# A graph network of four layers on one core: separate buffers for the attention outputs that the second attention projection loads, and v stored tile by tile

## The chip, the cores and the metric

The kernel runs on one core of one Trainium2 chip. The metric is the device time of one execution in microseconds (us), and lower is better. Times are medians of several executions. One further execution is recorded by the hardware profiler; the profile and the trace show that one.

## What is computed

The input is x with 2708 rows and 512 columns, and a symmetric 0/1 adjacency matrix of 2708 x 2708. Four layers follow each other, each as x = layernorm(x + layer(x)). Layers 0 and 1 sum neighbours through dense matrix products. Layers 2 and 3 are graph attention:

```python
def _layernorm(x):
    return (x - mean(x)) / sqrt(var(x) + 1e-5)

def gat_heads(x, adj, W, a):                    # W: [heads, 512, width]
    Wh  = einsum('nf,hfo->hno', x, W)           # the projection
    src = einsum('hno,ho->hn', Wh, a[:, :width])
    dst = einsum('hno,ho->hn', Wh, a[:, width:])
    e   = leaky_relu(src[:, :, None] + dst[:, None, :], 0.2)
    return softmax(where(adj > 0, e, -9e15)) @ Wh    # the attention, per head

# layer 2: 8 heads of 64
x = _layernorm(x + concat_heads(gat_heads(x, adj, W2, a2)))
# layer 3: 8 heads of 64, then one head of 512, then a two-layer MLP
h = elu(concat_heads(gat_heads(x, adj, W1, a1)))
h = elu(gat_heads(h, adj, Wo[None], ao[None])[0])
x = _layernorm(x + relu(h @ lin1_w + lin1_b) @ lin2_w + lin2_b)
```

## The kernel before

**Tiles and stages.** The 2708 rows are cut into NT = 22 tiles of 128 rows (the last has 20). The attention outputs are made in two blocks of 11 tiles each; `cuts` are their bounds. In time the kernel runs the layers 0 and 1 (to 889 us), the projection of layer 2 (889 to 981) and its attention (to 1531), the first projection of layer 3 (1531 to 1644) and its attention (to 2190), the projection to the single head of 512 (2190 to 2283; called layer 4's projection here), and its attention with the MLP (to 3004).

**The projection.** `project` is one function for all three projections. It loops over the 22 row tiles. For each tile t it takes the 128 rows of its input in SBUF from a function `source`, turns them with four TensorE transposes into PSUM (L124), copies these with ScalarE into a buffer `xT` (L126), and multiplies with the weight `w`: 16 matmuls (L627; four parts of the depth, twice over two halves of the columns) into the PSUM pair `pm`, of which there are two pairs. Of the two, 512 columns are Wh; 8 more columns in each half are the products with the attention vectors. From `pm` VectorE copies the `dst` column (L632) and a limited `src` column `b` (L634). ScalarE makes exponentials of them, `ecol` and `ucol` (L648, L649), VectorE multiplies Wh by `ecol` into the resident array `R2` (two L656; for the single head ScalarE does this), and ScalarE and GpSimd make `vcol` (L662) and `bcol` (L663). At the last tile of a block `split` cuts the block's exponentials into parts of lower precision (L560 to L564, L669, L672; some are casts on VectorE).

**The row v.** The attention needs exp of `b` as a row along the free axis, for all 128 partitions. `keep_v(t)`, called one tile late, transposes `b` (L604), takes the exponential with ScalarE into a row buffer `vrow` (L605), and at the last tile of a block stores this block's row to `v_dram` (L608, on SyncE's queue). The attention loads `v_bc` from there, a row of a block repeated on 128 partitions (`Weights.load`, L697, on SyncE's queue, 704 KB each). `Weights.first` is called by the projection at each tile: at tile NT - 8 it asks for two of these loads, and at tiles NT - 6 to NT - 3 it makes the first four arrays `e` of the attention (L703, VectorE), ordered by explicit dependencies between two tiles' products. Each `e` then gets its counterpart `c` by a sigmoid on ScalarE (L730), and the attention's matmuls are L895. At the end of each group of heads the attention stores its outputs to `o_dram` (L846, L848), and it stores the reciprocal sums in `rcs`.

**The source of layer 3's projection.** For layer 2 `source` is `plain`: it loads a tile of x2. For layer 3 it is `summed`: a load of the attention's outputs `o` (`fetched`, L164, 256 KB on SyncE's queue) and of x2 into a ring `spare` of two, then on VectorE o x rcs (L934) and + x2 (L935), and the layer norm in place:

```python
nc.vector.tensor_mul(by_head, by_head, rcs[...])              # L934
nc.vector.tensor_add(o, o, x2)                                # L935
layer_norm(late, o, n, o, on_scalar=True)
nc.gpsimd.dma_start(x3_dram[t * P:t * P + n, :], o)           # L937
return o
```

`layer_norm` computes statistics on VectorE (L108, L110, L112), takes the power -1/2 on GpSimd (L113), one more small step on VectorE (L117), and applies scale and bias with ScalarE (L118). The result x3 goes to `x3_dram` (L937, on GpSimd's queue) for the last layer's sum, and to the transposes L124. For layer 4's projection `elu_turned` loads the outputs already transposed, in pairs of tiles from tile 3 on, so that no transposes on TensorE are needed; SyncE issues these loads too.

**Buffers.** The pool `ahead` lives through the whole kernel. `fetched` takes its tiles there under the name `rows`, a ring of three, so that in layer 3's projection each `rows` buffer holds a tile from its load of o until its store of x3 and its transposes have ended. `xT` has two buffers in the same pool. The pool `sm` of a projection has two buffers of each name, unless told otherwise; `vrow` has one.

**Order.** The kernel is written as one program with all tiles' steps in a row. `early(first, n, make)` calls for the source of a tile one tile, and for its transposes none, ahead of the loop, and `xTs(t + 1)` is asked for ahead of tile t's matmuls. From that a scheduler makes one fixed list of instructions for each engine, and it sees the buffers: a step may be listed ahead only as far as there is a buffer for it. Each engine then executes its list in order, waiting on semaphores where data or a buffer are not ready; a DMA is started by the engine in whose list it stands. VectorE's list in layer 3's projection alternates between the steps of a tile's source (L934, L935 and the norm) and those that empty `pm` (L634, L632, L656). In the kernel before the source is three tiles ahead.

Of the kernel before, what the change touches and what calls it, by code (L numbers as in the profile page):

```python
# [9 lines left out]
F32 = mybir.dt.float32  # L10
# [3 lines left out]
AF = mybir.ActivationFunctionType  # L14
# [4 lines left out]
P = 128  # L19
D = 512  # L20
KD = D // P
EPS = 1e-5
ALPHA = 0.2
# [7 lines left out]
def kernel(  # L31
# [9 lines left out]
    nc = tc.nc  # L41
# [8 lines left out]
    def rows(t):  # L50
        return min(P, N - t * P)
# [34 lines left out]
    x2_dram = dram.tile([N, D], F32, name="x2_dram")  # L86
    x3_dram = dram.tile([N, D], F32, name="x3_dram")


    o_dram = dram.tile([N, D], F32, name="o_dram")  # L90
# [15 lines left out]
    def layer_norm(pool, y, n, dst, on_scalar=False):  # L106
        st = pool.tile([P, 6], F32, name="ln_st")
        nc.vector.bn_stats(st[:n], y)  # L108
        mv = pool.tile([P, 2], F32, name="ln_mv")
        nc.vector.bn_aggr(mv[:n], st[:n])  # L110
        rs = pool.tile([P, 1], F32, name="ln_rs")
        nc.vector.tensor_scalar(rs[:n], mv[:n, 1:2], EPS, None, op0=OP.add)  # L112
        nc.gpsimd.tensor_tensor(rs[:n], rs[:n], half[:n], OP.pow)  # L113
        if not on_scalar:
            nc.vector.tensor_scalar(dst, y, mv[:n, 0:1], rs[:n], op0=OP.subtract, op1=OP.mult)
            return
        nc.vector.scalar_tensor_tensor(mv[:n, 0:1], mv[:n, 0:1], -1.0, rs[:n], op0=OP.mult, op1=OP.mult)  # L117
        nc.scalar.activation(dst, y, AF.Identity, bias=mv[:n, 0:1], scale=rs[:n])  # L118
# [22 lines left out]
    ahead = fast.enter_context(tc.tile_pool(name="ahead", bufs=2))  # L141
# [7 lines left out]
    def early(first, n, make):  # L149

        made = {}

        def get(i, **how):
            for j in range(len(made), min(i + first + 1, n)):
                made[j] = make(j, **how)
            return made[i]
        return get
# [4 lines left out]
    def fetched(src, t, n, pool=ahead, name="rows", bufs=None):  # L162
        x_ = pool.tile([P, D], F32, name=name, bufs=bufs or (3 if pool is ahead else None))
        nc.sync.dma_start(x_[:n], src[t * P:t * P + n, :])  # L164
        return x_[:n]
# [28 lines left out]
    with ExitStack() as phase:  # L194
# [17 lines left out]
        sm = phase.enter_context(tc.tile_pool(name="l01", bufs=2))  # L212
# [22 lines left out]
        cuts = [(b, min(b + 4, NT)) for b in range(0, NT, 4)]  # L235
        cuts = cuts[-1:] + cuts[:-1]
# [38 lines left out]
        with ExitStack() as ph:  # L275
# [21 lines left out]
            for t in range(NT):  # L297
                n = rows(t)
# [29 lines left out]
        with ExitStack() as ph:  # L328
# [121 lines left out]
            for i, b in enumerate(cuts):  # L450
# [19 lines left out]
                for t in ts_:  # L470
                    n = rows(t)
# [9 lines left out]
            for t in range(NT):  # L481
                n = rows(t)
# [10 lines left out]
        with ExitStack() as ph:  # L493
            st = ph.enter_context(tc.tile_pool(name="l1b", bufs=2))
            for t in range(NT):
                n = rows(t)
# [17 lines left out]
    late = fast.enter_context(tc.tile_pool(name="late", bufs=1))  # L514
# [51 lines left out]
    def project(name, source, layer, v_dram, cuts, turned=None, first=None):  # L566


        w_src, w_view, _, heads = atts[layer]
# [9 lines left out]
        with ExitStack() as ph:  # L579
            sm = ph.enter_context(tc.tile_pool(name=f"{name}_s", bufs=2))  # L580
# [3 lines left out]
                           for k in (("pv", "pmm") if first else ("pmm", "pv")))  # L584
            if not first:
                ps_v, ps_mm = ps_mm, ps_v
            width = max(z - a for a, z in cuts) * P
            xs = early(1, NT, lambda t: source(sm, t, rows(t)))
            xTs = early(0, NT, lambda t: transposed(ahead, ps_tr, xs(t), rows(t), "xT"))
            if turned:  # L590
# [1 line left out]
                cuts_ = [(t, t + 1) for t in range(3)] + [(t, min(t + 2, NT)) for t in range(3, NT, 2)]  # L592
                parts = early(2, len(cuts_), lambda i: ready[i] if i in ready else turned(sm, *cuts_[i]))
                xTs = lambda t: parts(t if t < 3 else (t - 3) // 2 + 3)[:, :, ((t - 3) % 2 if t > 2 else 0) * P:][:, :, :P]
            vrows, bs, scaled = {}, {}, {}

            def keep_v(t):
                n = rows(t)
                a, z = next(c for c in cuts if c[0] <= t < c[1])
                if t == a:  # L600
                    vrows[a] = sm.tile([heads, width], F32, name="vrow", bufs=1)
                vrow = vrows[a]
                ps = ps_v.tile([P, P], F32, name="ps_v")
                nc.tensor.transpose(ps[:heads, :n], bs[t][:n, :heads], ident[:n, :n])  # L604
                nc.scalar.activation(vrow[:, (t - a) * P:(t - a) * P + n], ps[:heads, :n], AF.Exp, scale=ALPHA - 1.0)  # L605
                if t == z - 1:
                    cols = slice(a * P, a * P + (z - 1 - a) * P + n)
                    nc.sync.dma_start(v_dram[:, cols], vrow[:, :cols.stop - cols.start])  # L608

            for t in range(NT):  # L610
                n = rows(t)
# [17 lines left out]
                if t:  # L629
                    keep_v(t - 1)  # L630
# [34 lines left out]
                a, z = next(c for c in cuts if c[0] <= t < c[1])  # L665
                if t == z - 1:
                    if heads > 1:
# [3 lines left out]
                        for k in range(2):  # L671
                            nc.vector.tensor_scalar(pairs_c[:, a:z, :, k, 6 * k:6 * k + 3], parts_m[:, a:z, k::2, :],  # L672
                                                    -1.0, None, op0=OP.mult)
                            split(sm, pairs_c[:, a:z, :, k, 6 * k + 3:6 * k + 6], ecol[:, a:z, k::2])
            keep_v(NT - 1)
            sq = sm.tile([P, NT * H], F32, name="sq", bufs=1)[:, :NT * heads]
            dd = dcol[:, :, :heads]
# [56 lines left out]
    cuts = [-((-NT * i) // nb) for i in range(nb + 1)]  # L734
# [193 lines left out]

    def summed(sm, t, n):

        o, x2 = fetched(o_dram, t, n), fetched(x2_dram, t, n, late, "spare", 2)
        b = next(i for i, (a, z) in enumerate(blocks) if a <= t < z)
        by_head = o.rearrange("p (h c) -> p h c", h=H)
        nc.vector.tensor_mul(by_head, by_head, rcs[:n, b, :, t - blocks[b][0], None].to_broadcast([n, H, HO]))  # L934
        nc.vector.tensor_add(o, o, x2)  # L935
        layer_norm(late, o, n, o, on_scalar=True)
        nc.gpsimd.dma_start(x3_dram[t * P:t * P + n, :], o)  # L937
        return o

    loads, ready = [], {}  # L940

# [148 lines left out]
    for i, source in enumerate((plain, summed)):  # L1090
        with ExitStack() as ph:
            att = Weights(ph, f"a{2 + i}", blocks, vd[i])
            project(f"p{2 + i}", source, i, vd[i], blocks, first=att.first)
            heads_attention(f"a{2 + i}", att, i == 0, {
                9 + 4 * t: [lambda t=t: ready.update({t: elu_turned(None, t, t + 1)})] for t in range(3)} if i else {})
    ph4 = fast.enter_context(ExitStack())
    att = Weights(ph4, "a4", quads, vd[2])
    lin = ph4.enter_context(tc.tile_pool(name="lin", bufs=1)).tile([P, KD * FF + KF * D + KD * 512], F32, name="lin")
    scaled = project("p4", None, 2, vd[2], quads, elu_turned)


# [13 lines left out]
    def general(ctx):  # L1115
# [184 lines left out]
        def heads_attention(name, add):  # L1300

            with ExitStack() as ph:
# [51 lines left out]
                for b in range(nb):  # L1354
                    bc = att.load_shifts(b, 0)
                    for h in range(H):
                        nxt = att.load_shifts(b, h + 1) if h + 1 < H else None
                        main(b, h, bc, att.ahead(b + 1, h))
                        bc = nxt

        project("p2", lambda sm, t, n: None, l2_w, head_weights, head_vectors(l2_a), H)
        heads_attention("a2", add=True)
        project("p3", norm_and_keep, l3_w1, head_weights, head_vectors(l3_a1), H)
# [63 lines left out]
```

## Time and profile before

| | us |
|---|---|
| median of 3 runs | 3004.74 |
| lowest and highest | 3001.74, 3009.93 |
| profiled execution: its own time | 3005.91 |
| its span in the trace | 3004.1 |
| busy in the span: TensorE matmul (PE) | 2890.8 (96%) |
| TensorE weight load (PEld, beside PE) | 1608.9 (54%) |
| VectorE (DVE) | 1997.4 (66%) |
| ScalarE (ACT) | 1533.7 (51%) |
| GpSimd (POOL) | 251.0 (8%) |
| mean granted TensorE clock, 1 is full speed | 0.994 |

Busy times are sums over the whole span, while the stages differ: over the two attentions with 8 heads VectorE is nearly as busy as TensorE, in the projections it is not. The shares of a stage are therefore read from windows of the trace. A line of such a window has the start and end, the length, and for each engine its busy time and, in brackets, its number of instructions. In lines of the chain of waits and of the timeline, the first number is the start in us from the beginning of the span, the second the length; `out<-in` names what is written and read, and L12 is line 12 of the kernel. The trace leaves out the digits of names, so `x_dram<-rows` is here a store to `x3_dram`. SPq is SyncE's issuing of a DMA.

### The profile page before, as it was taken

Reading aid. Unit: us, or ns where it says so; the run is one execution under the profiler, and the core shown is the slowest. Engines: PE = TensorE matmul, PEld = TensorE weight load, DVE = VectorE, ACT = ScalarE, POOL = GpSimd, SP = SyncE. Lnnn points to the kernel's source line nnn. Section 1 sums busy time; section 2 is a strip of 40 time slices with the busy share of each in tenths; the row PEclk is TensorE's granted clock in tenths of the full one; section 3 lists DMA queues with packets and bytes.
Section 4 is the critical chain, followed back from the end, with each engine's and each line's share of the span. In section 5 each row is a group of like instructions: output and inputs, shape, how many; then the busy total and the mean of one; then the engine's idle time right before and its main releaser. Section 6 shows DMA issues by size and latency. Waiting matters only on the chain.

```text
span 3004.1 us, 36497 instructions
## 1 busy us (share of the span) xinstructions
PE 2890.8 (96%) x14456; PEld 1608.9 (54%) x14456; DVE 1997.4 (66%) x2405; ACT 1533.7 (51%) x1774; POOL 251.0 (8%) x341
## 2 busy tenths in 40 slices
PE   7999999999999999999998999999989999999998
PEld 3447766448888333444466334434465555555555
DVE  5975638512334999999976999999953535444342
ACT  3545543113224999999955899999941000000001
POOL 1110101201110000000022000000310000000000
PEclk9999999999999999999999999999999999999999
DMA  4533325422222011111144111121061000000000
GB/s 110 114 87 64 88 74 139 131 64 84 85 73 80 31 49 39 37 48 46 32 132 131 39 39 39 41 64 36 32 176 40 4 25 15 25 14 15 14 22 20
DMA packets 117426, 180.05 MB, mean 60 GB/s; under 512 B 41042, under 2 KB 65507, under 8 KB 117246
## 3 DMA queue, kind: packets, MB, share of 16 engines
q1 hardware_dynamic: 88974, 116.47, 13.3%
q0 software_dynamic: 18160, 57.39, 6.7%
q10 hardware_dynamic: 10112, 3.77, 0.5%
q8 instruction: 116, 1.90, 0.3%
q14 instruction: 64, 0.52, 0.1%
HBM read 147.55 MB, written 44.65 MB: 64 GB/s over the span
## 4 chain that ended last, share of the span: by engine, by line
PE 66%; DVE 19%; issue 6%; ACT 5%; DMA 3%; POOL 1%; SPq 0%; DVEq 0%; POOLq 0%; ACTq 0%
PE po L895 15%; PE pn L1056 13%; DVE e L703 10%; PE acc L506 7%; PE pm L228 7%; PE pm L627 6%; PE pl L1031 5%; PE pl L1022 5%; PE acc L460 4%; ACT c L730 3%; PE pd L799 2%; DVE places L252 2%; PE ps_tr L124 1%; DVE maskT L485 1%; DMA x_dram<-rows 0%
## 5 line engine op out<-in xcount | busy, mean ns | idle before, releaser
L703 DVE SCALAR_TENSOR_TENSOR e<-v_bc,ucol,maskT 128x1408 f32<-128x1408 f32 (+3 forms) x804 | 1136.4, 1475 | 326.1 <-PE pn L1056 315.5
L730 ACT ACTIVATE c<-e,bcol 128x1300 fp8e4<-128x1300 f32 (+1 forms) x688 | 967.7, 1423 | 75.5 <-DVE e L703 30.0
L895 PE MATMUL po<-e,R 128*64 128x512 f32 (+2 forms) x4224 | 904.1, 547 | 30.9 <-DVE e L703 27.5
L895 PEld LDWEIGHTS po<-e,R 128*64 128x64 f32 x4224 | 338.8, 136 | 563.1 <-issue 396.5
L1056 PE MATMUL pn<-e,R 128*128 128x512 f32 (+1 forms) x1056 | 413.5, 542 | 0.0
L1056 PEld LDWEIGHTS pn<-e,R 128*128 128x128 f32 x1056 | 191.0, 190 | 199.3 <-issue 196.1
L1024 ACT ACTIVATE w<-pl,b 128x256 f32<-128x256 f32 (+1 forms) x88 | 40.9, 465 | 372.9 <-PE pl L1022 364.8
L460 PE MATMUL acc<-yH,kT 128*128 128x512 f32 x484 | 198.3, 410 | 4.9 <-ACT kT L335 4.9
L228 PE MATMUL pm<-w,xT 128*128 128x512 f32 (+1 forms) x384 | 177.2, 605 | 23.1 <-DVE yL L223 19.7
L460 PE MATMUL acc<-yL,kT 128*128 128x512 f32 x484 | 190.3, 393 | 0.0
L506 PE MATMUL acc<-yH,mf 128*128 128x512 f32 x484 | 188.5, 389 | 0.0
L506 PE MATMUL acc<-yL,mf 128*128 128x512 f32 x484 | 188.3, 389 | 0.0
L627 PE MATMUL pm<-w,xT 128*128 128x264 f32 (+1 forms) x704 | 169.7, 395 | 2.9 <-DVE R L656 1.2
L228 PE MATMUL pm<-weight,xT 128*128 128x512 f32 (+1 forms) x352 | 161.9, 603 | 2.7 <-DVE u L317 1.9
L1031 PE MATMUL pl<-lin,w 128*128 128x512 f32 (+1 forms) x352 | 157.4, 592 | 0.0
L1022 PE MATMUL pl<-lin 128*128 128x256 f32 (+1 forms) x704 | 153.4, 371 | 3.7 <-DVE lin L924 3.7
L1022 PEld LDWEIGHTS pl<-lin 128*128 128x128 f32 x704 | 129.2, 190 | 34.4 <-issue 15.8
L627 PEld LDWEIGHTS pm<-w,xT 128*128 128x128 f32 (+1 forms) x704 | 131.2, 192 | 28.6 <-issue 2.4
L503 ACT CAST mf<-maskT 128x1024 fp32r<-128x1024 fp8e4 (+1 forms) x66 | 64.4, 977 | 158.0 <-PE acc L506 147.9
L222 ACT CAST yH<-pm 128x512 fp32r<-128x512 f32 (+1 forms) x44 | 25.7, 585 | 233.5 <-PE pm L228 233.5
L113 POOL TENSOR_TENSOR ln_rs<-ln_rs,half 128x1 f32<-128x1 f32 x88 | 57.5, 654 | 1019.6 <-DVE ln_rs L112 884.2
L335 ACT ACTIVATE kT<-maskT 128x512 fp32r<-128x512 fp8e4 (+1 forms) x132 | 77.6, 594 | 118.1 <-PE acc L460 118.1
(215 smaller groups left out, 2763.6 us busy)
## 6 DMA issues: line engine op xcount, KB each, us to landing
rows<-x_dram SPq DMA_DIRECT2D x63, 256.0 KB
v_bc<-v_dram SPq DMA_DIRECT2D x16, 704.0 KB
x_dram<-u POOLq DMA_DIRECT2D x42, 256.0 KB, 2.4
v_bc<-v_dram SPq DMA_DIRECT2D x16, 650.0 KB
m<-in_adj_dram POOLq DMA_DIRECT2D x13, 677.0 KB, 8.5
rows<-in_x_dram SPq DMA_DIRECT2D x21, 256.0 KB
r_dram<-u POOLq DMA_DIRECT2D x21, 256.0 KB, 3.3
rows<-r_dram SPq DMA_DIRECT2D x21, 256.0 KB
```

The lines of the kernel that those rows point to most:

```text
L228: order(nc.tensor.matmul(pm[:n], xT[:, k, :n], w[:, k, :], start=(k == 0), stop=(k == KD - 1)))
L335: made = nc.scalar.activation(kT[:, :w], maskT[:, j, b[0] * P:b[0] * P + w], AF.Relu, scale=-1.0)
L460: nc.tensor.matmul(pa[t], kT[:, (t - b[0]) * P:(t - b[0] + 1) * P], y[:, j, :], start=(j == 0 and y is yH), stop=(j == NT - 1 and y is yL))
L503: nc.scalar.copy(mf[:, :g1 - g0, :], maskT[:, g0:g1, t * P:(t + 1) * P])
L506: nc.tensor.matmul(pa, mf[:, j - g0, :], y[:, j, :], start=(j == 0 and y is yH), stop=(j == NT - 1 and y is yL))
L627: nc.tensor.matmul(pm[a][:m, :D // 2 + heads], xT[:, k, :m], w[:, k, a, :D // 2 + heads], start=(k == 0), stop=(k == KD - 1))
L703: self.made = nc.vector.scalar_tensor_tensor(e[:, :w], v[:, :w], ucol[:, j, h:h + 1], maskT[:, j, c0:c0 + w], op0=OP.max, op1=OP.mult)
L730: nc.scalar.activation(c[:, :w], e[:, :w], AF.Sigmoid, bias=bcol[:, j, h:h + 1], scale=STEP, saturate=False)
L895: pe(nc.tensor.matmul(po[i][HO * k:HO * k + HO, :c1 - c0], R2[:, j, h * HO:(h + 1) * HO], e[:, c0:c1], start=(i_ == 0), stop=(i_ == NT - 1)))
L1022: nc.tensor.matmul(pl[:, :w], self.lin1[:, k, f * P:(f + 1) * P], h[:, k, :w], start=(k == 0), stop=(k == KD - 1))
L1031: nc.tensor.matmul(pl[:n], gT[:, f, (t - t0) * P:(t - t0) * P + n], self.lin2[:, f, :], start=(f == 0), stop=(f == KF - 1))
L1056: nc.tensor.matmul(pn[k][:, :w], R2[:, j, k * P:(k + 1) * P], e[:, :w], start=(j == 0), stop=(j == NT - 1))
```

## The change

There are two parts, in three places of the code.

In `keep_v`, and so in all three projections, `vrow` is now a buffer of one tile's width (two of them, the pool's own number), and it is stored to `v_dram` for each tile as soon as its exponential is taken. The store is issued by ScalarE instead of SyncE. Before there were two stores in each of the projections with 8 heads and six in layer 4's, whose blocks (`quads`) have up to four tiles; now there are 22 in each. The computed width and the dictionary of rows are gone.

In `summed`, o is loaded, from tile 2 on, into a ring `o` of three buffers in the projection's pool, and the layer norm writes x3 from there into a new tile of the ring `rows`. Tiles 0 and 1 are as before.

```diff
@@ -584,7 +584,6 @@
                            for k in (("pv", "pmm") if first else ("pmm", "pv")))
             if not first:
                 ps_v, ps_mm = ps_mm, ps_v
-            width = max(z - a for a, z in cuts) * P
             xs = early(1, NT, lambda t: source(sm, t, rows(t)))
             xTs = early(0, NT, lambda t: transposed(ahead, ps_tr, xs(t), rows(t), "xT"))
             if turned:
@@ -592,20 +591,15 @@
                 cuts_ = [(t, t + 1) for t in range(3)] + [(t, min(t + 2, NT)) for t in range(3, NT, 2)]
                 parts = early(2, len(cuts_), lambda i: ready[i] if i in ready else turned(sm, *cuts_[i]))
                 xTs = lambda t: parts(t if t < 3 else (t - 3) // 2 + 3)[:, :, ((t - 3) % 2 if t > 2 else 0) * P:][:, :, :P]
-            vrows, bs, scaled = {}, {}, {}
+            bs, scaled = {}, {}
 
             def keep_v(t):
                 n = rows(t)
-                a, z = next(c for c in cuts if c[0] <= t < c[1])
-                if t == a:
-                    vrows[a] = sm.tile([heads, width], F32, name="vrow", bufs=1)
-                vrow = vrows[a]
+                vrow = sm.tile([heads, P], F32, name="vrow")
                 ps = ps_v.tile([P, P], F32, name="ps_v")
                 nc.tensor.transpose(ps[:heads, :n], bs[t][:n, :heads], ident[:n, :n])
-                nc.scalar.activation(vrow[:, (t - a) * P:(t - a) * P + n], ps[:heads, :n], AF.Exp, scale=ALPHA - 1.0)
-                if t == z - 1:
-                    cols = slice(a * P, a * P + (z - 1 - a) * P + n)
-                    nc.sync.dma_start(v_dram[:, cols], vrow[:, :cols.stop - cols.start])
+                nc.scalar.activation(vrow[:, :n], ps[:heads, :n], AF.Exp, scale=ALPHA - 1.0)
+                nc.scalar.dma_start(v_dram[:, t * P:t * P + n], vrow[:, :n])
 
             for t in range(NT):
                 n = rows(t)
@@ -928,14 +922,17 @@
 
     def summed(sm, t, n):
 
-        o, x2 = fetched(o_dram, t, n), fetched(x2_dram, t, n, late, "spare", 2)
+
+        o = fetched(o_dram, t, n) if t < 2 else fetched(o_dram, t, n, sm, "o", 3)
+        x2 = fetched(x2_dram, t, n, late, "spare", 2)
         b = next(i for i, (a, z) in enumerate(blocks) if a <= t < z)
         by_head = o.rearrange("p (h c) -> p h c", h=H)
         nc.vector.tensor_mul(by_head, by_head, rcs[:n, b, :, t - blocks[b][0], None].to_broadcast([n, H, HO]))
         nc.vector.tensor_add(o, o, x2)
-        layer_norm(late, o, n, o, on_scalar=True)
-        nc.gpsimd.dma_start(x3_dram[t * P:t * P + n, :], o)
-        return o
+        x3 = o if t < 2 else ahead.tile([P, D], F32, name="rows", bufs=3)[:n]
+        layer_norm(late, o, n, x3, on_scalar=True)
+        nc.gpsimd.dma_start(x3_dram[t * P:t * P + n, :], x3)
+        return x3
 
     loads, ready = [], {}
```

## The prediction, made before the changed kernel ran

> **What bounds the kernel now.** I read the busy table first, then the windows by stage, the chain of waits and the timeline of the stage that the change names. Below, t counts the 22 row tiles of layer 3's projection from 0; "front" of a tile is DVE's L934, L935 and the layer norm's four small steps, "back" is L634, L632 and the two L656.
>
> The windows (core, length, then PE, PEld, DVE, ACT and POOL busy, clock, DMA share, GB/s) of the projections of layers 2, 3 and 4:
>
> ```profile
> 880.00:985.00 105.00, 103.48 (x519) 84.25 (x519) 41.48 (x135) 47.38 (x126) 11.06 (x34) 1.00 0.27 83
> 1531.00:1645.00 114.00, 99.44 (x462) 78.47 (x462) 75.91 (x232) 59.84 (x145) 34.36 (x66) 0.96 0.48 153
> 2190.00:2283.00 93.00, 83.62 (x403) 67.99 (x399) 37.00 (x86) 39.02 (x125) 2.20 (x3) 0.94 0.60 154
> ```
>
> Layer 2's is full on PE (103.5 of 105 us). Layer 3's leaves PE idle for 14.6 us and runs at clock 0.96: there is something to win here. Layer 4's idle time lies at its beginning, where it waits for other loads. The attention after layer 3's projection is as full on DVE (528.2 of 535 us from 1655 to 2190) as on PE (520.1), so what the projection ends earlier is not taken back there by itself.
>
> The chain of waits of layer 3's projection (start, length, what):
>
> ```profile
> 1550.79 5.70 DMA x_dram<-rows
> 1556.62 2.63 DMA rows<-o_dram
> ...
> 1562.76 0.66 PE ps_tr L124 x4
> 1563.42 5.25 PE pm L627 x16
> 1568.78 0.44 PE ps_tr L124 x4
> 1569.21 3.56 PE pm L627 x16
> ...
> 1605.64 4.12 DMA x_dram<-rows
> 1609.83 5.01 DMA rows<-o_dram
> ...
> 1617.05 3.64 DMA x_dram<-rows
> ```
>
> A store of x3 is followed directly by a load of o into the same ring: the three buffers `rows` hold a tile from the load of o until its x3 has landed. Of the waiting itself the timeline says (last bracket: idle before, and for whom):
>
> ```profile
> 1559.37 0.69 DVE L934 TENSOR_TENSOR rows<-rows,rcs 128x512 f32<-128x512 f32 x1 [2.88 <-DMA rows<-o_dram]
> 1562.76 0.66 PE L124 MATMUL ps_tr<-ident,rows 128*128 128x128 f32 x4 [2.29 <-ACT rows L118]
> 1563.26 5.42 PE L627 MATMUL pm<-w,xT 128*128 128x264 f32 x16
> 1593.43 0.29 SPq L608 DMA_DIRECT2D v_dram<-vrow  x1
> 1613.53 0.66 PE L124 MATMUL ps_tr<-ident,rows 128*128 128x128 f32 x4 [3.38 <-ACT rows L118]
> ```
>
> A full tile on PE repeats every 4.11 us (1568.62, 1572.72, 1576.83, 1580.94). At that pace the stage would take 21 x 4.11 + 7.8 (last transposes and two tiles of matmuls) = 94.1 us; it takes 1644.3 - 1531.2 = 113.1. The 19.0 us lost: 4.5 up to tile 8 (1568.6 instead of 1564.1), none from tile 8 to 12, 12.6 from tile 12 to 21 (49.6 instead of 37.0), 1.9 after it. In the 12.6 are DVE's block of L560 to L672 casts after tile 10, v_bc loads of 704 KB ahead of tile loads, and ACT's table changes for L730.
>
> **What the Trainium skill says.** "DMA: Bandwidth & Descriptors", Anatomy of one DMA: a transfer has a fixed cost of about 2.0 us, mostly the receipt of the write. The trace agrees: L937's 256 KB land after 2.4 to 5.7 us, median 3.2. Same page, Issuing engines are not separate DMA queues: issuing from another engine only saves the time of the sequencer. Here that time is 0.27 us on SP (L608) and 0.33 us on ACT (L855). "TensorE: Matmul & The Clock Gate", What's actually happening: after some 3.4 us of idleness the clock is halved. Half agreed: after 3.1 us broken by one short transpose the clock of 1563 to 1568 was 0.66 and a tile took 5.42 instead of 3.73, yet after 3.4 us at 1610 the next one took 3.73.
>
> **The change part by part.**
>
> *Ring of o (t >= 2).* The load of o(t+3) no longer waits for the store of x3(t) but for ACT's L118(t). At L118(6) that is worth up to the 5.70 us above. New waits: L118(t) on x3(t-3) landed and its transposes done. The store is then three tiles (12.3 us) old against at most 5.7, so nothing; if it did wait, the xT copy and vcol behind it on ACT would be late, and PE with them. The ring costs something at the start: before, o(0), o(1) and o(2) were fetched ahead; now o(2) is issued behind the last o_dram stores (SP free at 1532.4). It lands 2.8 us later (as 1556.62 to 1559.37; bounds 2.4 and 5.1), at 1535.2. I followed the scheduled order by hand with the rows' durations: L118(2) 1539.7 (before 1535.8), transposes of tile 4 at 1549.2 (1547.7), but tile 7 at 1561 and tile 8 at 1565.2 (1568.6), without the cold tile. Gain there 3.4.
>
> *Order on DVE.* With three plus three buffers the program as it is scheduled has the front of tile 16 ahead of the back of tile 10; before it was three tiles ahead. DVE must keep that order. From L117(6) at 1555.9 to the end of back 10 this order has 9 fronts of 2.56 (0.69 x 3 + 0.18 + 0.15 + 0.16) and 7 backs of 0.95, 29.7 us, and 9 x 0.2 waiting for POOL's L113: 1587.4, against 1590.4 before. Then 3.2 of casts + 2.6 + 0.95: back 11 at 1594.1; 1.5 + 3.3 + 0.95: back 12 at 1599.8. Its PSUM frees the matmuls of tile 14. From there DVE needs 2.8 to 3.7 a tile and PE sets the pace again: 8 x 4.11 = 32.9, last matmul at 1632.7 instead of 1644.3. **Gain 11.6** for the whole projection, the 3.4 included.
>
> *v_bc.* SP issues them after o(19) instead of after o(14), some 10 us ahead of the first e; loads beside them took up to 5.1 us, so o(t) is safe. DVE makes one e more before the casts at the end: 1.7 gained.
>
> *v stores.* 66 on ACT for 10 on SP. SP no longer stands before L608 (1590.07 to 1593.43, the o load behind it): counted above. On ACT, 22 x 0.33 = 7.3 us a projection; layer 2's ACT is 47 of 105 us busy, layer 4's 39 of 93, and PE's 3.6 to 4.1 us a tile cover it. Only where ACT is full, at layer 2's end (22.9 of 25 us from 960 to 985), six stores add 2.0, against one pair of 1.28 us table loads now listed later: 1.0 lost, bounds -3 to +3. vrow(t) now waits for store t-2 to land: 8.2 us against some 3 (bounds 2.0, the fixed cost, and 5.7): nothing. Behind it on ACT are ecol, ucol and xT. Layer 4: nothing, bounds 1 either way; SP loses ten waits there, but its loads wait for rings.
>
> **Sum:** 11.6 + 1.7 - 1.0 = 12.3 us off the profiled execution's 3005.91 (span 3004.1), 2993.6. That execution stood 1.2 above the median of three, 3004.74; against the median 2992.4, say 2992.5.
>
> **Rivals.**
> A, the sum above, 9 to 20 us won (20: PE sets the pace from tile 8, ending at 1626.4, with the e and layer 2's bound). 2984 to 2995.7.
> B, another wait takes over, 0 to 9 won. If o(2) lands after 5.1 us and DVE keeps its order, back 10 is at 1589.7, the end at 1635; ACT's stores at both ends take 4: about 5 won, 2999.5. For it: DVE's fixed order. If the tail is ACT's (table loads of 1.28 us each) and not the loads', only the 3.4 at the start are won: 3001.3. Against it: SP's loads wait visibly at 1605 and 1617.
> C, slower: ACT becomes the queue that holds up. Each store waits there for its own vrow and, as scheduled, often for an earlier DMA of SP's; the next vrow but one waits for its landing. This decides once a v store lands later than two tiles, 8.2 us, or, in the three tails where stores are 3 to 4 us apart, later than about 4. Three late stores in each tail at 2 to 3 us are 18 to 27, less 12: 6 to 15 slower, about 3013. Against it: 4 KB beside 256 KB that land in 3.2.
> That the change doesn't do what it says is excluded: in the scheduled program the loads of o wait for ACT alone.
>
> **Numbers.** A 0.66, B 0.23, C 0.11. About 0.3% (9 us) is what this kernel's measurement can tell from no change; the bound between A and B is put there, and all of C is counted as slower, though its lower end (6 us) lies within it. The range 2984 to 3003 leaves out C, the top of B and a little below A.
>
> **What would show it.** Right: in the chain no x3 store ahead of an o load; L934 waiting under 4 us for loads (9.4 now); no tile of 5.4 at tile 7; the last L627 near 1633 and the first L895 near 1634; layer 2's and 4's windows as they were. Back 10 at 1587 and a gap of PE near 1595 to 1600 would confirm DVE's order as the next bound; a PE that runs through would give 20. Wrong: ACT idle before L605 for v_dram, or layer 2's projection longer by more than 3 us.

## The result, and the profile after

The changed kernel takes 2994.82 us (median of 7 runs, 2993.23 to 3000.23) against 3004.38 us (7 runs, 3000.83 to 3009.93). The ratio is 0.9971, 95% interval 0.9961 to 0.9981: 9.6 us or 0.3% faster: little, but the interval leaves out no change. A second set of runs (e9 below) gave the same ratio, 0.9971, interval 0.9959 to 0.9983. The forecast was 2992.5 us.

The profiled execution of the changed kernel took 2999.24 us (span 2997.4), that of the kernel before 3005.91 (3004.1): 6.7 us apart. Single executions differ by several us for a reason outside the change: in the profiles of all kernels here, layer 2's projection has its first L627 anywhere from 883.4 to 893.6 us. Stages are therefore compared by their lengths. The line numbers of the changed kernel are lower: what was L605, L608, L627, L703, L730 and L895 is L601, L602, L621, L697, L724 and L889. In tables and text the numbers of before stand for both.

The windows of the changed kernel (core, length, then PE, PEld, DVE, ACT, POOL busy, clock, DMA share, GB/s), the same three stretches as before:

```profile
880.00:985.00 105.00, 100.28 (x503) 83.03 (x501) 40.91 (x134) 47.72 (x125) 11.06 (x34) 0.99 0.28 83
1531.00:1645.00 114.00, 104.97 (x515) 80.71 (x516) 80.88 (x250) 68.45 (x160) 33.46 (x67) 0.99 0.54 169
2190.00:2283.00 93.00, 81.86 (x364) 64.69 (x363) 37.28 (x84) 37.06 (x118) 0.91 (x1) 0.94 0.61 152
```

In the second line PE is 5.5 us busier (104.97 instead of 99.44) and its clock 0.99 instead of 0.96: layer 3's projection is fuller, and in its place the attention already runs in the last 7 us of the window. The first line shows what was not expected: PE is busy for 3.2 us less in the stretch that ends layer 2's projection.

The chain of waits in layer 3's projection, after (start, length, what):

```profile
1548.88 0.82 ACT rows L118
1549.72 3.25 DMA o<-o_dram
...
1577.22 0.72 ACT rows L118
1577.96 3.61 DMA o<-o_dram
...
1587.70 0.82 ACT rows L118
1588.54 3.73 DMA o<-o_dram
```

A load of o now follows an L118, not a store of x3. (Two more loads of o are in the chain; the view puts a row of v ahead of them, also on ScalarE.) No store of x3 is left in the chain, which had three of them in this stage.

How long PE waits in this stage (waiting instruction, for whom, us in total, times, longest; the largest three of each kernel), first before, then after:

```profile
PE ps_tr L124 <- ACT rows L118: 7.9, 6, 3.4
PE ps_v L604 <- DVE b L634: 3.7, 3, 2.1
PE ps_v L604 <- ACT vrow L605: 1.5, 1, 1.5
```

```profile
PE ps_tr L124 <- ACT rows L118: 2.0, 3, 0.9
PE pm L621 <- ACT xT L126: 1.8, 2, 1.2
PE pm L621 <- DVE R L650: 1.4, 3, 0.6
```

The wait for x3 fell from 7.9 to 2.0 us. What remains is spread over several small waits.

And here is the loss, at the end of layer 2's projection. The timeline of ScalarE and of TensorE's first attention matmul before (start, length, engine, line, what; in the bracket idle before, and for whom):

```profile
980.57 0.27 ACT L605 ACTIVATE vrow<-ps_v 8x128 f32<-8x128 f32 x1
...
981.37 0.33 ACT L605 ACTIVATE vrow<-ps_v 8x128 f32<-8x128 f32 x2
981.72 1.28 ACT L730 ACT_TABLE_LOAD   x1
981.76 10.69 PE L895 MATMUL po<-e,R 128*64 128x512 f32 x50 [0.31 <-ACT vrow L605]
```

and after:

```profile
980.76 0.27 ACT L601 ACTIVATE vrow<-ps_v 8x128 f32<-8x128 f32 x1
...
981.56 0.27 ACT L601 ACTIVATE vrow<-ps_v 8x128 f32<-8x128 f32 x1
...
981.94 1.28 ACT L724 ACT_TABLE_LOAD   x1
983.23 1.47 ACT L724 ACTIVATE c<-e,bcol 128x1408 fp8e4<-128x1408 f32 x1
984.72 1.28 ACT L634 ACT_TABLE_LOAD   x1
...
986.19 0.16 ACT L601 ACTIVATE vrow<-ps_v 8x20 f32<-8x20 f32 x1
...
986.40 10.17 PE L889 MATMUL po<-e,R 128*64 128x512 f32 x38 [4.78 <-ACT vrow L601]
```

The rows of v of tiles 20 and 21 were made together before (the x2). Now the row of tile 21 stands behind a table load, a sigmoid c and another table load. PE's first attention matmul waits for this row in both kernels, 0.31 us before and 4.78 after. The buffer was not what ScalarE waited for: the store of tile 19, whose buffer the row of tile 21 takes, was issued at 981.05 and had landed at 982.26, by the trace's semaphores, and ScalarE shows no idle time between the rows. It only had other work first in its list.

In stage lengths (from the timelines; "again" is the profile of e9):

| stretch | before | after | again |
|---|---|---|---|
| last L627 of layer 2's projection to first L895 | 0.63 | 5.09 | 5.09 |
| last L627 of layer 2's to first L124 of layer 3's projection | 550.1 | 553.8 | 553.9 |
| layer 3's projection, first L124 to the end of the last L627 | 113.1 | 101.2 | 102.1 |
| from there to layer 4's first L627 | 547.1 | 546.8 | 546.6 |
| layer 4's first L627 to the first L1056 | 92.5 | 94.1 | 92.7 |
| from there to the end | 720.2 | 720.2 | 720.4 |

Won 11.0 to 11.9 us in layer 3's projection, lost 3.6 to 3.8 ahead of it. Layer 4's row is not a reading: it lies between 91.3 and 95.0 us in the profiles of the other kernels below whose attention is unchanged, without order.

### The profile page after: what moved, and what is told of

The parts are those of the page before. It is cut to its first block, busy times and chain, and to the rows that moved or that the text cites. A ratio compares the mean times of both kernels' runs of the same rounds, so it can differ in the third digit from the quotient of the medians.

```text
span 2997.4 us, 36576 instructions
## 1 busy us (share of the span) xinstructions
PE 2888.5 (96%) x14456; PEld 1607.6 (54%) x14456; DVE 1994.0 (67%) x2405; ACT 1535.3 (51%) x1772; POOL 217.5 (7%) x341
## 4 chain that ended last, share of the span: by engine, by line
PE 63%; DVE 19%; issue 7%; ACT 6%; DMA 3%; POOL 1%; SPq 0%; DVEq 0%; ACTq 0%; POOLq 0%
PE pn L1053 13%; PE po L889 13%; DVE e L697 12%; PE acc L506 7%; PE pm L228 7%; PE pm L621 5%; PE pl L1028 5%; PE pl L1019 5%; PE acc L460 4%; ACT c L724 4%; PE pd L793 2%; DVE places L252 1%; PE ps_tr L124 1%; DVE maskT L485 1%; DMA o<-o_dram 1%
## 5 line engine op out<-in xcount | busy, mean ns | idle before, releaser
L697 DVE SCALAR_TENSOR_TENSOR e<-v_bc,ucol,maskT 128x1408 f32<-128x1408 f32 (+3 forms) x804 | 1134.8, 1466 | 327.2 <-PE pn L1053 315.9
L724 ACT ACTIVATE c<-e,bcol 128x1300 fp8e4<-128x1300 f32 (+1 forms) x688 | 968.0, 1423 | 77.0 <-DVE e L697 33.1
L889 PE MATMUL po<-e,R 128*64 128x512 f32 (+2 forms) x4224 | 905.6, 548 | 32.8 <-DVE e L697 25.2
L889 PEld LDWEIGHTS po<-e,R 128*64 128x64 f32 x4224 | 339.8, 137 | 565.7 <-issue 396.9
L621 PE MATMUL pm<-w,xT 128*128 128x264 f32 (+1 forms) x704 | 166.6, 390 | 5.9 <-DVE R L650 2.5
L621 PEld LDWEIGHTS pm<-w,xT 128*128 128x128 f32 (+1 forms) x704 | 128.8, 188 | 30.7 <-ACT xT L126 4.9
```

The costliest lines, as they stand in the source:

```text
L621: nc.tensor.matmul(pm[a][:m, :D // 2 + heads], xT[:, k, :m], w[:, k, a, :D // 2 + heads], start=(k == 0), stop=(k == KD - 1))
L697: self.made = nc.vector.scalar_tensor_tensor(e[:, :w], v[:, :w], ucol[:, j, h:h + 1], maskT[:, j, c0:c0 + w], op0=OP.max, op1=OP.mult)
L724: nc.scalar.activation(c[:, :w], e[:, :w], AF.Sigmoid, bias=bcol[:, j, h:h + 1], scale=STEP, saturate=False)
L889: pe(nc.tensor.matmul(po[i][HO * k:HO * k + HO, :c1 - c0], R2[:, j, h * HO:(h + 1) * HO], e[:, c0:c1], start=(i_ == 0), stop=(i_ == NT - 1)))
```

## The experiments

Each diff is against the kernel named. "Gap" is the first row of the table above, "projection" the third, each from one profile; the three profiles with the same order of VectorE's steps in this stage (the change, e9 and e1) have 101.2, 102.1 and 102.2 us of projection. The total is a median, with the ratio to the kernel before and its interval. e1 to e4, e5 to e8 and e9 to e12 are three sets, each on its own chip beside the kernel before, whose medians there are 3004.46, 3001.99 and 3004.30 us; between sets, and with the first result, only ratios are compared.

**e1: per-tile v in layer 3 alone.** Against the changed kernel; the branch not shown is that of the kernel before:

```diff
+                by_tile = name == "p3"
...
-                nc.scalar.dma_start(v_dram[:, t * P:t * P + n], vrow[:, :n])
+                if t == z - 1:
+                    (nc.scalar if by_tile else nc.sync).dma_start(v_dram[:, cols], vrow[...])
```

> The changed kernel, but with v stored per block on SyncE's queue, as before, in the projections of layers 2 and 4; per tile on ScalarE's queue only in layer 3's. My theory: the changed kernel wins some 12 us in layer 3's projection and gives back about 4 at the end of layer 2's, where ScalarE takes the last row of v only after a sigmoid and two table loads, and TensorE's first L889 waits for it (4.78 us). Then the first attention matmul of layer 2 is back near 981.8 us (986.4 in the changed kernel), layer 3's projection keeps its gain, and the whole stands near 2991, 13 below the kernel before. Rival: the 4 us come from something else (the attention's own first tiles), then 2995 as the changed kernel. Second rival: stores on ScalarE also cost in layer 4's projection (94.1 us against 92.5), then near 2989.

Measured: gap 0.63 us, projection 102.2 us, 2993.07 us, ratio 0.9960 (0.9946 to 0.9973). The gap is gone and the gain kept. In this profile the attention's first matmul came at 976.5 and not at 981.8, because its layers 0 and 1 had ended 5 us sooner; the gap is what is to be read. The total lies halfway between the expected 2991 and the rival's 2995, and its interval overlaps that of the change, so the total does not tell the two apart.

**e2: the part on v alone.** `summed` as in the kernel before.

> Only the part on v: 22 stores per projection on ScalarE's queue; o loaded and normed in the ring rows as before. My theory: nothing of the gain is in this part. Layer 2's end loses the 4 us, layer 3's projection gets at most 3 us from SyncE no longer standing at the block's store (1590 to 1593) and loses 1 to 2 at its end: 3005 to 3008. Rival: the gain in layer 3's projection comes from SyncE's queue being free of the v store, not from the ring of o; then layer 3's projection is 6 or more us shorter and the whole is at 2998 to 3001.

Measured: gap 5.09 us, projection 106.8 us, 3005.12 us, ratio 1.0003 (0.9994 to 1.0011). The total is in the expected range, but the projection is 6.3 us shorter where at most 3 were expected: this part has a gain of its own there, which is lost again: 3.7 us ahead of that projection and 2.3 between it and layer 4's (second and fourth row of the table: 553.8 and 549.4 us). e5, e6 and e12 look for it.

**e3: three v rows.** Against the changed kernel:

```diff
-                vrow = sm.tile([heads, P], F32, name="vrow")
+                vrow = sm.tile([heads, P], F32, name="vrow", bufs=3)
```

> The changed kernel with three buffers vrow instead of two. My theory: what makes the last row late is the ring of two, whose buffer for tile 21 is free only when the store of tile 19 has landed; the scheduler therefore puts a sigmoid with its table loads ahead of it. With three it stands directly behind tile 20's row: the first attention matmul of layer 2 at 982 to 983 instead of 986.4, total near 2990.5. Rival: it is ScalarE's issuing of stores (0.27 us each, and waiting for the queue) that costs; that is the same here, so 2995 and a first matmul at 986.

Measured: gap 0.73 us, first attention matmul at 982.3, projection 102.3 us, 2992.91 us, ratio 0.9953 (0.9940 to 0.9967). Its timeline at the same place:

```profile
981.83 0.27 ACT L601 ACTIVATE vrow<-ps_v 8x128 f32<-8x128 f32 x1
982.00 0.19 ACT L656 ACTIVATE vcol<-b 20x8 f32<-20x8 f32 x1
982.10 0.16 ACT L601 ACTIVATE vrow<-ps_v 8x20 f32<-8x20 f32 x1
982.12 0.27 ACTq L602 DMA_DIRECT2D v_dram<-vrow  x1
982.31 3.87 PE L889 MATMUL po<-e,R 128*64 128x512 f32 x18 [0.41 <-ACT vrow L601]
```

With one buffer more, the row of tile 21 directly follows that of tile 20, and 0.2 us later PE starts. All the stores are still issued by ScalarE.

**e4: per-tile v on SyncE.** Against the changed kernel:

```diff
-                nc.scalar.dma_start(v_dram[:, t * P:t * P + n], vrow[:, :n])
+                nc.sync.dma_start(v_dram[:, t * P:t * P + n], vrow[:, :n])
```

> The changed kernel with the per-tile stores of v issued by SyncE instead of ScalarE; two buffers as in the change. By my theory (the ring of two decides) the first attention matmul of layer 2 still waits for the last row and comes at 985 to 987. By the rival (ScalarE's queue decides) it is back near 982. In layer 3's projection SyncE stands before each v store with o loads behind it: I expect 2 to 6 us longer there than in the changed kernel, total 2997 to 3001; if the queue does not matter there, 2995.

Measured: gap 5.04 us, projection 102.0 us, 3000.91 us, ratio 0.9986 (0.9979 to 0.9994). The gap stays when the stores leave ScalarE's queue, and in e3 it goes although they stay there: the ring of two is its cause. The expected 2 to 6 us of SyncE's queue in the projection did not come: with o loaded well ahead, SyncE may stand. They came behind it instead, where the attention of layer 3 begins 5.0 us after the last L627 (1.6 in the change), since here tile 21's row stands behind a table load, a sigmoid and another table load there too. By layer 4's projection 2.7 us of that are left (549.5 us in the fourth row, 546.8 in the change).

**e5: the ring of o alone.** Against the kernel before, `summed` as in the change, and, for room, fewer buffers in the attentions:

```diff
-            c = self.pool.tile([P, self.W], F8, name="c", bufs=11)
+            c = self.pool.tile([P, self.W], F8, name="c", bufs=8)
```

> The ring of three for o alone; v stored per block on SyncE's queue, as before, in all projections. Two whole vrow rows and the ring do not fit together, so the attention's ring c has 8 buffers here instead of 11; only the projections are read, not the total. My theory now: the ring of o is enough by itself for layer 3's projection, first transpose to last L627 in 101 to 103 us (113.1 before, 101.2 in the change), and layer 2's end is as before (0.6 us from the last L627 to the first attention matmul). Rival: SyncE standing at the v store with o loads behind it, which in the other half of the change alone was worth 6.3 us, costs here too: 105 to 108 us.

Measured: gap 0.63 us, projection 103.5 us; total 3005.88 us, ratio 1.0011 (1.0003 to 1.0019), with attentions 3 to 5 us longer each (552.5 and 549.9 us, from the first attention matmul to the next projection), which is put down to the fewer c, the only edit there. The projection is just above the expected 101 to 103 us. The ring alone gives 9.6 of the 11.9 us. SyncE's block store then costs at most 2.3, not the 4 to 7 of the rival.

**e6: the block store on ScalarE.** Against the kernel before:

```diff
-                    nc.sync.dma_start(v_dram[:, cols], vrow[:, :cols.stop - cols.start])
+                    nc.scalar.dma_start(v_dram[:, cols], vrow[:, :cols.stop - cols.start])
```

> The kernel before with one word changed: v is still stored per block, but by ScalarE instead of SyncE. The part on v alone made layer 3's projection 6.3 us shorter (106.8 instead of 113.1 us). Theory: that is SyncE no longer standing at the block's store ahead of o loads; then this word gives it too, 106 to 109 us, with layer 2's end as before, and the total is 3 to 6 below the kernel before. Rival: it came from the scheduler's other order of VectorE's list or from how long the stores of x3 happened to take (5.70 us once before); then this kernel's projection is anywhere from 109 to 114 us.

Measured: gap 0.63 us, projection 111.4 us, 3001.06 us, ratio 0.9997 (0.9989 to 1.0006). Taking SyncE away from the block's store is worth 1.7 us in the profile and nothing in the total. The theory falls: the queue alone is not what gave e2 its 6.3. The rival, the order of VectorE's list or the time that stores of x3 happened to take, is left standing.

**e7: six buffers, all in place.** Against the changed kernel:

```diff
-        o = fetched(o_dram, t, n) if t < 2 else fetched(o_dram, t, n, sm, "o", 3)
+        o = fetched(o_dram, t, n) if t < 3 or t % 2 else fetched(o_dram, t, n, sm, "o", 3)
...
-        x3 = o if t < 2 else ahead.tile([P, D], F32, name="rows", bufs=3)[:n]
+        x3 = o
```

> The changed kernel, but even tiles from 4 on are loaded and normed in place in the ring o, odd tiles in place in the ring rows: the same six buffers, each held from the load of o until the store of x3 has landed. If the number of buffers decides, layer 3's projection takes 101 to 103 us as in the change. If the point is that loads of o have a ring of their own that no store holds, a load waits here for a store again, but for one six tiles old: I expect no more than 2 us longer. A rival against both: VectorE's list runs more tiles ahead here (six instead of five), so the emptying of pm is later and TensorE loses 3 to 5 us in the middle of the stage: 104 to 106.

Measured: gap 5.09 us (as in the change), projection 100.4 us, 2992.06 us, ratio 0.9967 (0.9954 to 0.9980). Once both rings are full, every load of o waits for a store of x3 again, one that is six tiles old, and the projection is no longer for it. The third expectation, that a longer lead of VectorE's list costs TensorE 3 to 5 us, fell too: L930 runs up to seven tiles ahead of L628 here, six in the change. The waits for loads of o on VectorE are even shorter:

```profile
DVE o L930 <- DMA o<-o_dram: 2.0, 2, 1.1
DVE rows L930 <- DMA rows<-o_dram: 0.3, 1, 0.3
```

**e8 and e10: more v rows, and o(2) fetched ahead.** Against the changed kernel:

```diff
-                vrow = sm.tile([heads, P], F32, name="vrow")
+                vrow = sm.tile([heads, P], F32, name="vrow", bufs=3 if name == "p3" else 8)
...
-        o = fetched(o_dram, t, n) if t < 2 else fetched(o_dram, t, n, sm, "o", 3)
+        o = fetched(o_dram, t, n) if t < 3 else fetched(o_dram, t, n, sm, "o", 3)
...
-        x3 = o if t < 2 else ahead.tile([P, D], F32, name="rows", bufs=3)[:n]
+        x3 = o if t < 3 else ahead.tile([P, D], F32, name="rows", bufs=3)[:n]
```

> The changed kernel with eight vrow buffers in the projections of layers 2 and 4 and three in layer 3's, and with o of tile 2 fetched into rows ahead of time, as before the change. Theory: the first part wins the 4.5 us at layer 2's end (first attention matmul 0.7 us behind the last L627, not 5.1), the second 1.5 to 3.5 us at the start of layer 3's projection (98 to 100 us instead of 101 to 102): total 2988 to 2990. Rival: the start is set by SyncE's loads behind the last attention stores and not by tile 2; then the projection stays at 101 to 102 and the total at 2991 to 2993.

Measured: gap 0.73 us, projection 98.3 us, 2987.35 us, ratio 0.9954 (0.9940 to 0.9967). The same once more beside the change:

> The version of e8 once more beside the change. The traces say 4.4 us less at layer 2's end, 2.9 in layer 3's projection, some 7 in all, of which the attention of layer 2 gives 0.8 back: 6 us below the changed kernel. If the two medians differ by under 3 us, the trace of e8 was a lucky one.

Measured: gap 0.72 us, projection 99.6 us, 2990.70 us, ratio 0.9952 (0.9939 to 0.9966). In e10 its slowest run (2991.84) is below the fastest of the changed kernel in e9 (2993.18). So this version beats both kernels, 5.5 us below the change by medians. Its transposes of tile 2 begin 7.2 us after the first (10.8 in the change). e3, without o(2) ahead, has the same ratio, so what the second edit adds to the total is in the profiles (2.6 to 4.0 us of projection) but not told apart by the times.

**e9: the changed kernel again.**

> The changed kernel itself once more, so that it stands beside the version of e8 on the same chip. Expected: layer 3's projection 100 to 103 us, 5 us between the last L627 of layer 2's projection and the first attention matmul, 8 to 11 us below the kernel before. If its first profile was a lucky or unlucky one, these two lengths move by more than 1.5 us.

Measured: gap 5.09 us, projection 102.1 us, 2996.18 us beside 3004.30 of the kernel before: 8.1 us.

**e11: two buffers of o.** Against the changed kernel:

```diff
-        o = fetched(o_dram, t, n) if t < 2 else fetched(o_dram, t, n, sm, "o", 3)
+        o = fetched(o_dram, t, n) if t < 2 else fetched(o_dram, t, n, sm, "o", 2)
```

> The changed kernel with two buffers in the ring o instead of three. If the number of buffers a load of o can run ahead into decides: o(t+2) now waits for the norm of tile t, about 0.8 us of ScalarE, 3.3 of load and 2.7 of VectorE for every other tile, 6.8 of the 8.2 us that TensorE needs for two; the chain just fits but has no slack for a late load, so layer 3's projection takes 104 to 108 us. If the freedom from the store decides (a load waits for ScalarE alone), 101 to 103 as with three.

Measured: gap 5.09 us, projection 108.8 us, 3004.03 us, ratio 1.0000 (0.9991 to 1.0008); the projection is just above the expected 104 to 108. PE's wait in its projection (same columns as above):

```profile
PE ps_tr L124 <- ACT rows L118: 9.2, 16, 1.3
```

The loads wait for ScalarE alone here, no store stands between, and yet most tiles make PE wait again, 16 times, where the changed kernel has 3. VectorE's list is another one too: L930 runs only two or three tiles ahead of L628, where the kernel before has three or four and the change up to six. So this run does not change the buffer alone.

**e12: per-tile v on SyncE, without the ring of o.** Against e2, the one word of e4.

> The part on v alone, with the per-tile stores on SyncE. With ScalarE's queue layer 3's projection took 106.8 us, with one block store on ScalarE 111.4. If the shorter hold of a per-tile store matters, and not the queue, 106 to 108 here; if it is SyncE's freedom that matters, 111 to 115, since SyncE now stands 22 times before a v store with loads of o behind it.

Measured: gap 5.04 us, projection 110.5 us, 3006.12 us, ratio 1.0003 (0.9994 to 1.0012). Between the two expectations, so it decides nothing by the total. The starts of tile 8's transposes, counted from the first transpose, say more: 37.4 us before and 37.0 in e6, but 34.6 in e2 and 33.6 in e12. The two kernels that store tile by tile, on whichever queue, are about 3 us sooner at tile 8, by one profile each. From there to the end e2 takes 72.2 us, e12 76.9 and the kernel before 75.7, so after tile 8 the gain is in e2 only. Why the first 3 come, I have not found: VectorE's list in e2 differs from that of the kernel before by one tile of lead in a few places, and no run separates that.

## Why the prediction was right, and where it was not

**The projection, 11.6 us: right, by its steps up to tile 10 and by luck after it.** Counted from the first L124, the working had the transposes of tiles 4, 7 and 8 at 18.0, 29.8 and 34.0 us and the emptying of tile 10 at 56.2 (1587.4). The trace has 17.7, 30.0, 34.1 and 56.5 (1590.80 + 0.76, from 1535.07). Then two errors cancel. Tile 12 was to be emptied at 68.6 and is at 65.7; from there the last matmul was to take 32.9 us and takes 35.5. So the end, forecast at 101.5, is at 101.2. The second profile repeats it: 56.3, 65.4, then 36.7 to the end at 102.1.

Two statements of the working go with this. VectorE's order as the next bound was to show as a gap of PE between tile 10 and tile 12. The gap is not there: from 1569.0 to 1600.8 PE is busy for 30.4 of 31.8 us, it waits for L650 only 0.65 and 0.31 us ahead of the casts and 0.43 us for a cast, and from 1596.30 to 1608.5 it runs through. And PE does not set the pace alone after that: it is busy for 33.0 of the last 35.5 us. The longest wait there is for the turned tile `xT`, whose copy stands on ScalarE behind a sigmoid c and two table loads of 1.28 us:

```profile
1619.69 3.83 PE L621 MATMUL pm<-w,xT 128*128 128x264 f32 x16 [1.23 <-ACT xT L126]
```

This is part of what the prediction named under B, a tail that is ScalarE's; there it was to take most of the projection's gain, here it took little of it.

The tile of 5.42 us is gone. The clock of 0.66 that the prediction read there is a mean: from 1563.76 to 1567.17 the trace has 0.50, and full clock on both sides. Before, there was such a stretch at the beginning of the stage too (1533.04 to 1536.45); the changed kernel has only that one (1536.55 to 1539.96).

**The reason for it was half right.** The prediction named the loads' freedom from the store. e7 makes the loads wait for stores again and keeps the gain (100.4 us), but these stores are six tiles old, about 25 us at PE's pace, where stores of x3 took 2.4 to 5.7 us to land before the change. e11 keeps the freedom, with a buffer less, and loses most of the gain (108.8 us). So the freedom alone does not give the gain, and with enough buffers it is not needed. What goes with the gain is how many tiles may be between the load of o and the end of its use, and with that how far ahead of L634 the scheduler lists the L934: three or four tiles before, up to six in the change, up to seven in e7. The number of buffers alone does not order the runs: e11 has five of them and the shortest lead, two or three tiles, since only two can be filled ahead by a load. That it is still 4.2 us shorter than the kernel before may be the freedom after all; no run holds the order of the list and changes the buffers, so these are not told apart.

**A mark that misled.** I gave as a sign "L934 waiting under 4 us for loads (9.4 now)". It is 7.1 us in the changed kernel:

```profile
DVE o L930 <- DMA o<-o_dram: 7.1, 9, 1.8
```

The waits are nearly as long, but they fall on a tile that PE needs several tiles later, so they no longer reach PE. The wait to watch was PE's for L118 (7.9 to 2.0).

**Layer 2's end, 1.0 us with bounds -3 to +3: mis-sized, and for a wrong reason.** It cost 4.5 us in the gap and 3.6 to 3.8 by the start of layer 3 (the attention gets 0.7 to 0.8 back). The prediction counted the table loads that come later as a gain of ScalarE's time. It did not ask what had changed places with them: the last row of v, read from PSUM, for which PE's first attention matmul waits, 0.31 us already in the kernel before. Nor does its sum come out: six stores at 0.33 us against a pair of table loads of 1.28 us each would be 0.6 won, not 1.0 lost. This is rival C's mechanism (the next row but one waits for a store) in one of its three tails. The point I set for it, stores later than about 4 us, was the wrong question: the stores need not be late at all, and were not: they landed 1.2 us after their issue for tile 19 and 1.06 to 5.70 us in all three projections, median 2.1, where the prediction took 2.0, the fixed cost that it cites, as the least and some 3 as usual. It was enough that the scheduler, with two buffers, put another instruction first. The sign I gave for it, ScalarE idle ahead of the row, could not show it either: ScalarE was busy with that other instruction.

**The e made sooner, 1.7 us: 0.3 to 0.5.** That is the difference in the whole fourth row of the stage table; how much of it is the e, no run shows. **Layer 4: nothing, bounds 1.** The second profile shows 0.2 us; the 1.6 of the first lie outside the bounds, but are of the size by which this stage varies. In sum 11.0 to 11.9, + 0.3 to 0.5, - 3.6 to 3.8, which is 8.5 us in the first profile and 7.8 in the second; the medians say 9.6 and 8.1 against the forecast's 12.3. Against the forecast's terms, layer 2's end is 2.6 to 2.8 us worse and the e are 1.2 to 1.4.

**What the part on v is for.** By itself it changes the total by nothing (e2, e12). With the ring of o it makes no difference to the projection on which queue v is stored (e4), and little whether by tile (e5, 1.4 to 2.3 us). What it does is to free memory: a row of a block is 11 x 128 x 4 = 5632 bytes in each partition's space, two tiles' rows are 1024, and the ring of o takes 3 x 2048.

**Left open.** Where e2's 3 us by tile 8 come from; how much of the ring's gain is the loads' freedom and how much the longer lead of VectorE's list; and whether a wider ring of o would bring the projection below the 98.3 to 99.6 us of e8 (at PE's own pace it would be 94.1, the prediction's estimate). The last was not tried.

## What to carry to other kernels

When a long row buffer is cut into small ones with a ring, ask for the last tiles of the stage what may overtake the step that waits for a buffer, and which engine's first work of the next stage waits for that step: one buffer more cost 512 bytes of each partition here and took 4.4 us out of the gap. When loads wait for stores of the same ring, count how many tiles the ring lets be under way before blaming the store, and look how far ahead the list then runs: six buffers gave the gain in two different layouts, a ring of their own with only two gave 4.2 of the 11 to 12 us. And read the waits of the engine that sets the pace; a wait of a helper engine may stay as long as it was and cost nothing.

## What the runs showed that was not expected

The two halves of the change do not add: alone they shorten the projection by 6.3 us (e2) and 9.6 us (e5), together by 11.0 to 11.9 us. And 22 issues of stores on ScalarE in a projection, with a median of 0.27 us each, hardly show in the stage that TensorE fills: layer 2's projection takes 90.90 us from its first to its last L627, 90.76 before.
